# A scan block on one NeuronCore: the tail behind the last pair, reordered over other PSUM banks

## The chip, the core and the metric

The kernel runs on one core of one Trainium2 chip. Its time is the device time of one execution in microseconds (us); lower is better. Five engines work side by side and wait for each other through semaphores: TensorE (PE in the profile, with PEld for its weight loads), VectorE (DVE), ScalarE (ACT), GpSimd (POOL), and SyncE (SP), which issues the transfers. TensorE writes its results to PSUM, which the kernel uses as one tile of eight banks, `psum[128, 8, 512]`. Only VectorE and ScalarE read these banks here; GpSimd works on SBUF alone.

## The reference, cut to what matters

The input `x` is (4, 128, 96, 96). It is group-normalized, read as four sequences of 9216 positions per image (rows forward and reversed, columns forward and reversed), and each sequence goes through one block:

```
t = grouped1x1(x, in_proj)            # 512 channels: u, gate
u = depthwise_conv(silu(u), 5 taps)
s, a, b, c = ssm_in(u), decay(u), tanh(ssm_b(u)), tanh(ssm_c(u))     # 32 channels each
h[l] = a[l] * h[l-1] + b[l] * s[l]    # the recurrence along the sequence
u = u + ssm_out(c * h + d * s)        # 32 -> 256 channels
y = out_proj(mix(u * sigmoid(gate)))  # 256 -> 128
```

The four results are joined by a 1x1 convolution (`fuse`) and added to `x`. The kernel keeps the sum of all four in `acc` and merges mix, out_proj and fuse into one matrix per direction, `w_fin`.

## The kernel before, in words

The work is cut into 384 units: 8 phases (4 images, columns then rows), 6 steps in a phase, 4 interleaved positions `p` in a step, and 2 sequences `s` (one forward, one reversed). Two units that differ only in `s` are a pair; a tile holds N = 384 positions. `pair(t)` runs 192 times. It makes the front of pair t (projection, convolution, `proj`) and the back of pair t - 6: so when the loop ends, six pairs still lack their back. These are pairs 186 to 191, that is units 372 to 383, and `tail()` (L893 to L986) finishes them. The order of the work is written out by hand: each engine executes its instructions in the order in which the code issues them, and a wait holds all that is queued behind it on that engine.

The back of one pair (units bi and bi + 1, with bi even) has these steps; the names are used below.

- **Scan** (`scan`, L702, VectorE): the recurrence over one step's 4 pairs, on partitions 64 to 127 of `t0`, in two halves of 768 elements. The second half starts from the last value of the first.
- **Outputs** (`outputs`, L708 and L709): z = c * h + d * s, a multiplication and an addition over 64 x 384, both of whose inputs lie in SBUF. They run on GpSimd, or on VectorE where `engine` says so.
- **z copy**: z is copied from partitions 0 to 63 to 64 to 127, since the four matmuls that follow use four different groups of 32 rows. It runs on GpSimd (L711, inside `outputs`) or on ScalarE (`z_copy`, L904).
- **Seed** (`under`, L505, ScalarE): u is copied into two PSUM banks, so that the matmuls add onto it.
- **State result** (`out_of`, L497, TensorE, called by `ssm_out` L898): 4 matmuls of 32 rows onto the seeds, for s = 0 into banks SSM and SSM + 1 (0 and 1), for s = 1 into banks 2 and 3.
- **Gating** (`gating`, L577, VectorE; L959 for the last pair in quarters): v = (g + 1) * state result, from the two banks to SBUF. It frees the two banks for the seed of the next pair.
- **Product** (`accumulate`, matmuls of L134 with `w_fin`): 8 matmuls of 32 columns give y of one unit in one bank. The profile counts each float32 matmul twice, so a product shows as 16.
- **Add** (`accumulate`): y goes into `acc`. Either ScalarE copies it to `ys` (L735, L737) and GpSimd adds that (L754), or, where `last` is set, VectorE adds straight from the bank (L752, L754). This frees the product's bank.

In the tail the state results of every pair use banks 0 to 3 and the products banks 4 to 7, in turn (`finish`, L914). The order on TensorE, as the built program has it, is: state result 186, products 370 and 371, state result 187, products 372 to 375, state results 188 and 189, products 376 and 377, state result 190, products 378 and 379, state result 191, products 380 and 381, and units 382 and 383 in four half products. Outputs 376 (pair 188) run on VectorE with their z copy on GpSimd; outputs 378, 380 and 382 run on GpSimd with their z copies on ScalarE. Between the scan's two halves stand state result 187 and the gating of pair 187.

Finished rows of `acc` are sent by `send()` (L717), and the last four pieces by L986.

Of the kernel before, what the change touches and what calls it, by code (L numbers as in the profile page):

```python
# [47 lines left out]
P = 128  # L48
# [14 lines left out]
UB = 8  # L63
# [4 lines left out]
def conv_preact_kernel(  # L68
# [418 lines left out]
    def gate(bi, s, j, to):  # L487
# [3 lines left out]
        nc.tensor.matmul(bank(to)[:, :N], stats[un["b"]][0][r, s, :], x_in[s][r, q, off : off + N],  # L491
                         start=True, stop=True)

    def out_of(bi, s, j):
        z = tbs[bi]
        r = slice(64 * j + 32 * s, 64 * j + 32 * s + 32)
        nc.tensor.matmul(bank(SSM + 2 * s + j)[:, :N], w_so[r, bass.ts(j, P)], z[r, :],  # L497
                         start=bi not in seeded, stop=True, skip_group_check=True)

    seeded = set()  # L500
# [1 line left out]
    def under(bi, s):  # L502

        seeded.add(bi)
        nc.scalar.copy(psum[:, SSM + 2 * s : SSM + 2 * s + 2, :N], us[bi][:, s])  # L505

    def sigmoids(bi, to):
        bn = stats[units[bi]["b"]][1]
# [57 lines left out]
    def gating(bi, s):  # L566

        v = units[bi + s]["v"] = us[bi][:, s]
        m = mirror(bi // 2)
        if m is None:  # L570
            g = gates[bi // 2 % 2][:, s]
        else:
            g = old_gates.get(bi // 2, gates[m % 2])[:, 1 - s, :, ::-1]
        pz = psum[:, SSM + 2 * s : SSM + 2 * s + 2, :N]
        if bi not in seeded:
            nc.vector.tensor_add(pz, pz, v)
        nc.vector.scalar_tensor_tensor(v, g, 1.0, pz, ALU.add, ALU.mult)  # L577
# [125 lines left out]
            seq[64:P, r], seq[64:P, r], seq[0:64, r], init, ALU.mult, ALU.add  # L703
        )

    def outputs(i, copy=nc.gpsimd.tensor_copy, engine=nc.gpsimd):
        ta, tb, p = scans[units[i]["step"]], tbs[i], units[i]["p"]
        engine.tensor_mul(ta[0:64, p, :], tb[64:P, :], ta[64:P, p, :])  # L708
        engine.tensor_add(tb[0:64, :], ta[0:64, p, :], tb[0:64, :])  # L709
        if copy:  # L710
            copy(tb[64:P, :], tb[0:64, :])  # L711

# [180 lines left out]
    def tail():  # L893
# [12 lines left out]
        def gate_units(n):  # L906
            for s in range(2):
                gating(2 * n, s)
                under(2 * n + 2, s)
                if s == 0 and n > first + 1:  # L910
                    z_copy(n + 1)
            waiting.extend(units[2 * n : 2 * n + 2])

        def finish(n):  # L914
            banks = (4, 5) if n % 2 else (6, 7)
            accumulate(waiting.pop(0), banks[0])()
            wait.append(accumulate(waiting.pop(0), banks[1], nc.vector, True))

        def add():
            if wait:  # L920
                wait.pop(0)()
            send()

        z_copy(first + 1)
        ssm_out(first)
        gate_units(first)
        for bk in (4, 5):
            accumulate(waiting.pop(0), bk)()
        scan(NU // UB - 1, 0)
        scale_s(NU - 2)  # L930
        ssm_out(first + 1)
        gate_units(first + 1)
        scan(NU // UB - 1, 1)
        outputs(2 * first + 4, nc.gpsimd.tensor_copy, nc.vector)
        outputs(2 * first + 6, None)
        for bk in (6, 7):
            wait.append(accumulate(waiting.pop(0), bk, nc.vector, True))
        for n in range(first + 4, end):
            outputs(2 * n, None)
        finish(first + 1)  # L940
        add()
        add()
        ssm_out(first + 2)
        for n in range(first + 2, end - 1):
            gate_units(n)
            add()
            if n > first + 2:
                finish(n - 1)
            ssm_out(n + 1)
        last = 2 * (end - 1)  # L950
        half = N // 2
        for s in range(2):
            bu = units[last + s]
            v = us[last][:, s]
            g = old_gates[last // 2][:, 1 - s, :, ::-1]
            for e in range(2):
                r = bass.ts(e, half)
                pz = psum[:, SSM + 2 * s : SSM + 2 * s + 2, r]
                nc.vector.scalar_tensor_tensor(v[:, :, r], g[:, :, r], 1.0, pz, ALU.add, ALU.mult)  # L959
        add()  # L960
        finish(end - 2)
        add()
        for s in range(2):
            bu = units[last + s]
            v = us[last][:, s]
            for e in range(2):
                r = bass.ts(e, half)
                py = bank(4 + 2 * s + e)
                for j in range(2):
                    for c in range(4):  # L970
# [202 lines left out]
```

## Time and profile before

| quantity | value |
|---|---|
| median of 3 runs | 1819.84 us (1818.55 to 1820.01) |
| the profiled execution, its own time | 1821.96 us |
| its span, first to last instruction | 1820.2 us |
| tail on TensorE (first product after pair 191's matmuls to the last matmul's end) | 1783.57 to 1815.24 us |
| last addition into `acc` ends | 1815.66 us |
| TensorE busy from 1784.5 to 1791.3 us | 6.61 of 6.80 us |
| ScalarE, VectorE, GpSimd busy over the span | 86%, 80%, 78% |

A row of the timeline reads: start in us from the span's beginning, duration in us, engine, source line, operation, what it writes and reads, shapes, and count; in brackets the idle time of the engine before it and what ended that time. Successive matmuls of a kind are merged into one row, which lasts from the first start to the last end, so waits inside such a row are not seen as idle time. In the view of windows each row gives a stretch, its length, the busy time and the number of instructions of each engine, and the TensorE clock that was granted (1.00 is full).

### The profile page before, as it was taken

The page shows a single profiled execution, that of the slowest core. Times are in us where ns is not written, and L with a number is a line of the kernel's source. Part 1 is how long each engine was busy: PE and PEld are TensorE (multiplying, and loading weights), DVE is VectorE, ACT ScalarE, POOL GpSimd, SP SyncE. Part 2 cuts the span into 40 slices and gives each one's busy share as a digit, 9 for nine tenths or more (in the row PEclk, how much of TensorE's full clock was granted, in tenths as well). Part 3 has the DMA queues.
Part 4 walks back from the last instruction along what each step waited for, and adds up shares of the span by engine and source line. Part 5 has one row for each costly group of instructions (what it writes and reads, how often), then busy time and mean ns, then how long its engine had stood idle before and what let it go on. Part 6 is the DMA issues. An engine that isn't in the chain of part 4 may idle for free.

```text
span 1820.2 us, 56934 instructions
## 1 busy us (share of the span) xinstructions
PE 1792.3 (98%) x24074; PEld 645.5 (35%) x24074; DVE 1454.6 (80%) x1462; ACT 1562.5 (86%) x2748; POOL 1428.2 (78%) x1475
## 2 busy tenths in 40 slices
PE   6999999999999999999999999999999999999998
PEld 3333333333333333333333333333333333333333
DVE  6888878877888888877778888887877788778885
ACT  4888888988988888888888888888888888888974
POOL 3587878778778888788877888887877888887785
PEclk9999999999999999999999999999999999999999
DMA  8555463444975465334696456453477644635434
GB/s 246 175 190 179 149 203 99 162 142 154 313 242 181 158 196 171 119 135 137 224 296 227 141 179 210 119 171 110 161 237 223 227 148 129 197 102 177 149 125 155
DMA packets 148047, 321.17 MB, mean 176 GB/s; under 512 B 14160, under 2 KB 115920, under 8 KB 147792
## 3 DMA queue, kind: packets, MB, share of 16 engines
q1 hardware_dynamic: 147648, 317.48, 54.2%
q8 instruction: 190, 3.11, 0.7%
q14 instruction: 65, 0.53, 0.1%
q10 hardware_dynamic: 144, 0.04, 0.0%
HBM read 185.21 MB, written 132.25 MB: 174 GB/s over the span
## 4 chain that ended last, share of the span: by engine, by line
PE 94%; ACT 2%; DVE 2%; DMA 1%; issue 0%; SPq 0%; POOL 0%; DVEq 0%; ACTq 0%; POOLq 0%
PE psum L134 81%; PE psum L497 8%; PE psum L491 5%; DMA xs<-in_xr 1%; ACT psum L505 1%; ACT sil L470 1%; DVE psum L630 1%; DMA acc<-in_xr 0%; DVE bn L298 0%; ACT u L611 0%; DVE u L577 0%; DVE u L630 0%; ACT psum L628 0%; DVE t L702 0%; SPq L296 0%
## 5 line engine op out<-in xcount | busy, mean ns | idle before, releaser
L630 DVE SCALAR_TENSOR_TENSOR psum<-sil,small,psum 128x768 f32<-128x768 f32 x576 | 589.0, 1023 | 28.8 <-ACT psum L628 3.4
L134 PE MATMUL psum<-u,w_fin 128*32 128x384 f32 x6176 | 553.1, 488 | 0.2 <-ACT t L673 0.2
L577 DVE SCALAR_TENSOR_TENSOR u<-gate,psum 128x768 f32<-128x768 f32 x376 | 349.8, 952 | 249.0 <-ACT gate L514 107.2
L134 PE MATMUL psum<-u,main 128*32 128x384 f32 x6144 | 534.9, 489 | 1.6 <-DVE u L630 1.5
L754 POOL TENSOR_TENSOR acc<-ys,acc 128x384 f32<-128x384 f32 x374 | 410.7, 1120 | 32.1 <-ACT ys L735 10.8
L708 POOL TENSOR_TENSOR t<-t,t 64x384 f32<-64x384 f32 x191 | 232.3, 1216 | 153.8 <-DVE t L702 70.2
L134 PEld LDWEIGHTS psum<-u,w_fin 128*32 128x32 f32 x6176 | 188.9, 110 | 322.4 <-issue 216.6
L134 PEld LDWEIGHTS psum<-u,main 128*32 128x32 f32 x6144 | 181.9, 109 | 328.4 <-issue 200.7
L505 ACT COPY psum<-u 128x768 f32<-128x768 f32 x352 | 276.7, 799 | 23.1 <-DVE u L630 11.3
L134 PE MATMUL psum<-sil,band 128*32 128x384 f32 x3072 | 285.2, 488 | 0.0
L675 POOL TENSOR_SCALAR t<-tm 64x384 f32<-64x384 f32 x191 | 177.2, 928 | 123.2 <-ACT tm L667 104.2
L709 POOL TENSOR_TENSOR t<-t,t 64x384 f32<-64x384 f32 x191 | 246.8, 1292 | 15.0
L497 PE MATMUL psum<-t,main 32*128 32x384 f32 x1536 | 242.1, 514 | 3.3 <-ACT psum L505 2.6
L628 ACT ACTIVATE psum<-sil,small 128x768 f32<-128x768 f32 x191 | 173.2, 907 | 61.1 <-DVE u L577 52.8
L514 ACT ACTIVATE gate<-psum,bnorm 128x384 f32<-128x384 f32 x384 | 192.1, 582 | 30.1 <-PE psum L491 28.6
L676 POOL TENSOR_TENSOR t<-t,tm 64x384 f32<-64x384 f32 x192 | 195.1, 1016 | 15.3
L630 DVE SCALAR_TENSOR_TENSOR u<-sil,small,psum 128x768 f32<-128x768 f32 x192 | 194.9, 1015 | 7.8
L470 ACT ACTIVATE sil<-psum,bnorm 128x385 f32<-128x385 f32 x384 | 192.1, 585 | 3.7 <-PE psum L134 1.5
L134 PE MATMUL psum<-sil,less 64*32 64x384 f32 x3072 | 168.1, 495 | 0.0
L491 PE MATMUL psum<-x_in,wn 32*128 32x384 f32 x768 | 157.4, 526 | 3.0 <-DVE shift L249 1.4
L711 POOL COPY t<-t 64x384 f32<-64x384 f32 x188 | 141.2, 751 | 15.5 <-PE psum L134 3.6
L134 PEld LDWEIGHTS psum<-sil,band 128*32 128x32 f32 x3072 | 90.3, 109 | 169.6 <-issue 94.4
(102 smaller groups left out, 1484.3 us busy)
## 6 DMA issues: line engine op xcount, KB each, us to landing
sil<-sil SPq DMA_DIRECT2D x128, 770.0 KB, 6.8
kept<-gate SPq DMA_DIRECT2D x80, 768.0 KB, 3.7
gate<-kept SPq DMA_DIRECT2D x76, 768.0 KB, 5.1
x_in<-in_xs SPq DMA_DIRECT2D x192, 96.2 KB, 2.5
out<-acc SPq DMA_DIRECT2D x48, 384.0 KB, 8.0
acc<-in_xr SPq DMA_DIRECT2D x39, 384.0 KB, 6.9
xs<-in_xr SPq DMA_DIRECT2D x72, 192.0 KB, 5.5
x_in<-in_xs SPq DMA_DIRECT2D x46, 192.5 KB, 3.5
```

The source lines that it names most:

```text
L134: nc.tensor.matmul(o[r, : rhs.shape[-1]], lhsT, rhs, start=start, stop=stop, skip_group_check=True)
L470: nc.scalar.activation(sils[step][:, s, j, g, :], bank(bk)[:, : N + 1], AF.Silu, bias=bn[:, 1:2] if j else bn[:, 4 + g : 5 + g],)
L491: nc.tensor.matmul(bank(to)[:, :N], stats[un["b"]][0][r, s, :], x_in[s][r, q, off : off + N], start=True, stop=True)
L497: nc.tensor.matmul(bank(SSM + 2 * s + j)[:, :N], w_so[r, bass.ts(j, P)], z[r, :], start=bi not in seeded, stop=True, skip_group_check=True)
L505: nc.scalar.copy(psum[:, SSM + 2 * s : SSM + 2 * s + 2, :N], us[bi][:, s])
L514: nc.scalar.activation(gv[:, s, j, :], bank(to[2 * s + j])[:, :N], AF.Tanh, bias=bn[:, 2 + j : 3 + j], scale=0.5,)
L577: nc.vector.scalar_tensor_tensor(v, g, 1.0, pz, ALU.add, ALU.mult)
L630: nc.vector.scalar_tensor_tensor(us[i][:, :, 1, :] if k == K - 1 else part, src, w_tap[:, k : k + 1], part, ALU.mult, ALU.add,)
L676: nc.gpsimd.tensor_mul(ta[0:64, p, :], tb[0:64, :], tm[0:64, :])
L708: engine.tensor_mul(ta[0:64, p, :], tb[64:P, :], ta[64:P, p, :])
L709: engine.tensor_add(tb[0:64, :], ta[0:64, p, :], tb[0:64, :])
L754: adder.tensor_add(part, y, part)
```

## The change

Everything outside `tail()` issues the same instructions as before. In the tail:

- The state results of the last four pairs (188 to 191) turn through three pairs of banks, 6 and 7, 0 and 1, 2 and 3, one pair of banks for each unit (`ssm`). The products use banks 4 and 5 alone, 4 for s = 0 and 5 for s = 1.
- The two halves of the last scan stand together, ahead of the gating of pair 187. Behind each half follow the outputs of 376 for that half of the positions, on GpSimd.
- Outputs 378 move from GpSimd to VectorE. The z copy of 376 moves from GpSimd to ScalarE.
- GpSimd's addition of 371 is issued behind the outputs of 376 instead of ahead of them.
- Product 372 no longer goes straight from the bank through VectorE, but through ScalarE's `ys` and a GpSimd addition, as all s = 0 products now do; s = 1 products are added by VectorE.
- On TensorE, state results and products alternate: 372, 373, 374, state result 188, 375, 376, state result 189, 377, 378, state result 190, 379, 380, state result 191, 381, then the four half products, in banks 4, 2, 3 and 6.
- On ScalarE each z copy stands behind both seeds of its pair.

```diff
+    turning = (6, 0, 2)
+    def ssm(bi, s):
+        k = bi - NU + 8 + s
+        return turning[k % 3] if bi >= NU - 8 else SSM + 2 * s
...
-        nc.tensor.matmul(bank(SSM + 2 * s + j)[:, :N], w_so[r, bass.ts(j, P)], z[r, :],
+        nc.tensor.matmul(bank(ssm(bi, s) + j)[:, :N], w_so[r, bass.ts(j, P)], z[r, :],
...
-    def outputs(i, copy=nc.gpsimd.tensor_copy, engine=nc.gpsimd):
+    def outputs(i, copy=nc.gpsimd.tensor_copy, engine=nc.gpsimd, r=slice(0, N)):
...
-        engine.tensor_mul(ta[0:64, p, :], tb[64:P, :], ta[64:P, p, :])
-        engine.tensor_add(tb[0:64, :], ta[0:64, p, :], tb[0:64, :])
+        engine.tensor_mul(ta[0:64, p, r], tb[64:P, r], ta[64:P, p, r])
+        engine.tensor_add(tb[0:64, r], ta[0:64, p, r], tb[0:64, r])
...
-                if s == 0 and n > first + 1:
-                    z_copy(n + 1)
-            waiting.extend(units[2 * n : 2 * n + 2])
-
-        def finish(n):
-            banks = (4, 5) if n % 2 else (6, 7)
-            accumulate(waiting.pop(0), banks[0])()
-            wait.append(accumulate(waiting.pop(0), banks[1], nc.vector, True))
+
+        def product(n, s, bk):
+            if s == 0:
+                accumulate(units[2 * n], bk)()
+            else:
+                wait.append(accumulate(units[2 * n + 1], bk, nc.vector, True))
...
         gate_units(first)
-        for bk in (4, 5):
-            accumulate(waiting.pop(0), bk)()
-        scan(NU // UB - 1, 0)
+        first_add, second_add = (accumulate(waiting.pop(0), bk) for bk in (4, 5))
+        first_add()
         scale_s(NU - 2)
+        for part in range(2):
+            scan(NU // UB - 1, part)
+            outputs(2 * first + 4, None, r=bass.ts(part, N // 2))
         ssm_out(first + 1)
+        second_add()
         gate_units(first + 1)
-        scan(NU // UB - 1, 1)
-        outputs(2 * first + 4, nc.gpsimd.tensor_copy, nc.vector)
-        outputs(2 * first + 6, None)
-        for bk in (6, 7):
-            wait.append(accumulate(waiting.pop(0), bk, nc.vector, True))
+        outputs(2 * first + 6, None, nc.vector)
+        product(first, 0, 4)
+        product(first, 1, 5)
+        z_copy(first + 2)
+        product(first + 1, 0, 4)
         for n in range(first + 4, end):
             outputs(2 * n, None)
-        finish(first + 1)
-        add()
         add()
         ssm_out(first + 2)
         for n in range(first + 2, end - 1):
             gate_units(n)
+            z_copy(n + 1)
+            product(n - 1, 1, 5)
             add()
-            if n > first + 2:
-                finish(n - 1)
+            product(n, 0, 4)
             ssm_out(n + 1)
...
-        add()
-        finish(end - 2)
+        product(end - 2, 1, 5)
         add()
...
-                py = bank(4 + 2 * s + e)
+                py = bank((4, 2, 3, 6)[2 * s + e])
```

More of the change, by code (lines that the diff above doesn't have):

```diff
@@ L504, in under @@
         seeded.add(bi)
-        nc.scalar.copy(psum[:, SSM + 2 * s : SSM + 2 * s + 2, :N], us[bi][:, s])
+        nc.scalar.copy(psum[:, ssm(bi, s) : ssm(bi, s) + 2, :N], us[bi][:, s])
     def sigmoids(bi, to):
@@ L573, in gating @@
             g = old_gates.get(bi // 2, gates[m % 2])[:, 1 - s, :, ::-1]
-        pz = psum[:, SSM + 2 * s : SSM + 2 * s + 2, :N]
+        pz = psum[:, ssm(bi, s) : ssm(bi, s) + 2, :N]
         if bi not in seeded:
@@ L909, in gate_units @@
                 under(2 * n + 2, s)
-                if s == 0 and n > first + 1:
-                    z_copy(n + 1)
-            waiting.extend(units[2 * n : 2 * n + 2])
-        def finish(n):
-            banks = (4, 5) if n % 2 else (6, 7)
-            accumulate(waiting.pop(0), banks[0])()
-            wait.append(accumulate(waiting.pop(0), banks[1], nc.vector, True))
+        def product(n, s, bk):
[3 more added lines that the diff above has]
+                wait.append(accumulate(units[2 * n + 1], bk, nc.vector, True))
         def add():
-            if wait:
-                wait.pop(0)()
+            wait.pop(0)()
             send()
@@ L957, in tail @@
                 r = bass.ts(e, half)
-                pz = psum[:, SSM + 2 * s : SSM + 2 * s + 2, r]
+                pz = psum[:, ssm(last, s) : ssm(last, s) + 2, r]
                 nc.vector.scalar_tensor_tensor(v[:, :, r], g[:, :, r], 1.0, pz, ALU.add, ALU.mult)
-        add()
-        finish(end - 2)
+        product(end - 2, 1, 5)
         add()
```

## The prediction

> **What bounds the kernel now.** I read the page's busy shares and chain first:
>
> ```profile
> span 1820.2 us, 56934 instructions
> ...
> PE 94%; ACT 2%; DVE 2%; DMA 1%; issue 0%; SPq 0%; POOL 0%; DVEq 0%; ACTq 0%; POOLq 0%
> ```
>
> TensorE is the chain for 94% of the span; outside the tail it is busy almost without a break, and the change leaves that part alone. So the question is what TensorE does behind pair 191. Its timeline there:
>
> ```profile
> 1788.07 5.37 PE L134 MATMUL psum<-u,w_fin 128*32 128x384 f32 x64
> 1793.44 1.49 PE L497 MATMUL psum<-t,main 32*128 32x384 f32 x8
> 1796.95 2.79 PE L497 MATMUL psum<-t,main 32*128 32x384 f32 x8 [2.02 <-ACT psum L505]
> 1799.66 5.35 PE L134 MATMUL psum<-u,w_fin 128*32 128x384 f32 x32
> 1804.94 0.93 PE L497 MATMUL psum<-t,main 32*128 32x384 f32 x8
> 1805.80 2.79 PE L134 MATMUL psum<-u,w_fin 128*32 128x384 f32 x32
> 1808.52 1.41 PE L497 MATMUL psum<-t,main 32*128 32x384 f32 x8
> 1809.85 5.39 PE L134 MATMUL psum<-u,w_fin 128*32 128x384 f32 x96
> ```
>
> Four products (x64) take 5.37 us, so one takes 1.29 us; a state result that waits for nothing holds TensorE for 0.86 us (1804.94 to 1805.80). Behind state result 188 TensorE has nothing left: result 189 needs the banks that gating 188 has yet to read. It idles 2.02 us and is then held again inside the row of 1796.95. And two products that take 2.79 us at 1805.80 took 5.35 us at 1799.66. The view of windows says why:
>
> ```profile
> 1791.30:1794.70 3.40, 3.39 (x36) 1.25 (x28) 2.92 (x5) 0.58 (x1) 1.17 (x2) 1.00 0.31 125
> 1794.70:1798.10 3.40, 1.38 (x9) 0.60 (x6) 2.28 (x3) 2.01 (x3) 3.17 (x4) 1.00 0.02 5
> 1798.10:1805.00 6.90, 6.90 (x41) 1.94 (x40) 1.91 (x2) 2.63 (x4) 5.25 (x5) 0.51 0.25 95
> ```
>
> The column behind the last bracket is the granted clock. After a stretch with TensorE busy for 1.38 of 3.40 us (41%) it ran at half clock for 6.9 us, which costs half of that, 3.4 us.
>
> **What could be had.** From 1788.07 the work is ten products (12.9), four state results (3.4) and four half products (2.6), with about 0.3 for the last matmul to end: 19.2 us, done at 1807.3. It ended at 1815.24 (1809.85 + 5.39). So 7.9 us are lost: 3.4 to the clock, 4.5 to waits. Nothing in the change can gain more.
>
> **The change, part by part.**
>
> *Alternation and turning banks.* With products 375 and 376 between state results 188 and 189, TensorE has 2 x 1.29 = 2.58 us of work while the chain to the next state result runs. That chain is gating of s = 0 (0.95), seed (0.80), z copy and TensorE's wake-up:
>
> ```profile
> 1796.00 0.80 ACT L505 COPY psum<-u 128x768 f32<-128x768 f32 x1 [3.21 <-DVE u L577]
> 1796.83 0.51 ACT L904 COPY t<-t 64x384 f32<-64x384 f32 x1
> ```
>
> The matmul of 1796.95 starts 0.15 us after that seed ends. So 0.05 + 0.95 + 0.05 + 0.80 + 0.03 + 0.51 + 0.15 = 2.54 us, hidden by 2.58 with nothing to spare; I allow 0.05 us of waiting in each of three rounds. The seed of s = 0 goes to banks already free and is done before. Bank 5 is freed by VectorE's additions (0.55), which end a microsecond before the next product needs it, bank 4 by `ys` (0.58) likewise. Under these covers both cost nothing.
>
> *Product 374* is the exception. It needs bank 4, and the `ys` of 372 stands on ScalarE behind the seed of 376 s = 1, which now waits for gating 374, which stands behind the second scan half. By rows: scan halves 1785.43 to 1787.25 and 1787.28 to 1789.1, gating to 1790.1, seed to 1791.0, `ys` to 1791.6, product 374 at 1791.7 instead of 1790.65: about 1 us of TensorE. What comes next swallows it.
>
> *Outputs 376 on GpSimd.* This is what decides. The four half operations have no row. Rows of GpSimd at other sizes:
>
> ```profile
> L226 POOL TENSOR_TENSOR inv<-inv,err 128x2 f32<-128x2 f32 x9 | 1.8, 196 | 0.7
> L1057 POOL TENSOR_TENSOR w_of<-w_of 128x512 f32<-128x512 f32 x1 | 1.3, 1278 | 8.0 <-ACT sil L470 8.0
> L1057 POOL TENSOR_TENSOR w_of<-w_of 128x256 f32<-128x256 f32 x1 | 0.7, 737 | 0.1
> ```
>
> These lie on a line from a base of 0.196 us. A whole output operation takes 1.19 (L708 in the tail), so a half is bounded by 0.60 (no base) and 1.19 (all base), and I take 0.196 + 0.99/2 = 0.69 us, with gaps of 0.08. Beside them stands this, from an earlier step:
>
> ```profile
> 1752.51 1.19 POOL L709 TENSOR_TENSOR t<-t,t 64x384 f32<-64x384 f32 x1
> 1752.52 2.80 DVE L702 TENSOR_TENSOR_SCAN t<-t,t 64x768 f32<-64x768 f32 x1
> 1753.77 1.86 POOL L711 COPY t<-t 64x384 f32<-64x384 f32 x1
> ```
>
> The scan, 1.81 us alone, took 2.80: it stood until GpSimd's operation ended. The copy, 0.50 alone, took 1.86: it stood until the scan ended, and finished 0.3 us later (its own time less 0.2). A scan and a GpSimd operation take turns. In the tail before, GpSimd had almost nothing to do beside the second half and VectorE's outputs. Now:
>
> - GpSimd's addition of 370, ready at 1787.85, stands until the scan ends at 1789.1, and ends at 1789.1 + 1.0 - 0.2 = 1789.9.
> - First half: multiplication to 1790.7, addition to 1791.45.
> - VectorE's outputs of 378 (0.89 each) come up at 1791.05. Whether they too take turns with GpSimd no row shows: the lower bound is no hold (gating rows beside GpSimd keep their 0.95), the upper that of the scan. I take turns, since like the scan they read two operands from SBUF and the gating reads one. So VectorE multiplies to 1792.15, GpSimd to 1792.65, VectorE adds to 1793.35, GpSimd to 1793.85. Without turns it would be 1793.0.
>
> The GPSIMD Engine Reference, Key points, says the same in general: GpSimd shares its SBUF interfaces with VectorE, with contention where VectorE reads two inputs from SBUF. By that rule 1814.5 us comes out, by free running 1813.7.
>
> Then the z copy ends at 1794.4, the waiting matmuls go on at 1794.55, and TensorE is free for 375 at 1795.4. Before, state result 188 ended at 1794.93; it comes no earlier now. The gain comes from what follows it.
>
> *The rest.* From 1795.4: five products (6.45), three state results (2.58), three waits (0.15), then two products and the four halves as before (5.39): 1795.4 + 14.57 = 1809.97. Before: 1815.24. The difference is **5.3 us**. Behind the last matmul everything stays: additions, the last transfers, 5.0 us to the span's end. On GpSimd three additions (1.08 each with the gap) and outputs 380 and 382 (1.27 an operation) follow 1793.85, so these end at 1799.6 and 1802.2; their z copies are due near 1800.8 and 1804.5. The transfers of finished rows move earlier and collide with nothing: the last ones still wait for the last additions.
>
> The span falls from 1820.2 to 1814.9; the profiled execution (1821.96, 1.7 us around the span) stands 2.1 us above the median. Taken from the median: 1819.84 - 5.3 = **1814.5 us** (-0.29%). A measurement of this kernel can tell about 0.2% (3.6 us) from no change.
>
> **The rivals.**
>
> *Half clock again.* In the window from 1791.3 to 1794.7 TensorE has product 374 (1.5 us) and the first part of state result 188 (0.7): busy about 65%. Below is the 41% that lost the clock; above, an early stretch that kept it:
>
> ```profile
> 16.40:19.80 3.40, 2.41 (x6) 0.78 (x5) 3.23 (x7) 0.00 (x0) 0.00 (x0) 1.00 1.05 286
> ```
>
> That is 71%. 65% is nearer to that, but no row tells which stretches the clock gate weighs. If the clock falls once: 1814.5 + 3.4 = 1817.9 us, no difference that counts. The same would come near if halves cost whole operations (up to 1.2 to 2.6 us more). The page TensorE: Matmul & The Clock Gate has the throttle fall only after an idle window of about 3.4 us; the trace lost its clock with 2.02 us idle at most, so the measurement decides. But its section "A second HAM failure mode: psum-queue depth-cycling" speaks against this change: turning through PSUM banks left TensorE with micro-idles and a clock that swung. By that section the sum would be 1817.9 or more.
>
> *GpSimd and VectorE do not hold each other up.* Then outputs 376 end at 1793.0 with only the scan's hold, giving 1813.7; with no hold at all at 1792, product 374 is the only wait, giving 1812.9.
>
> *Slower: the clock stays half.* If each round leaves TensorE below the share that lost the clock, three stretches of 6.9 us in a row cost 10.2 us: 1814.5 + 10.2 = 1824.7. It decides from the third stretch on (two give 1821.3). Against it: in the half-clock stretch before, TensorE was busy 6.90 of 6.90 us and got the clock back; a round of 3.44 us at full clock lasts 6.9 at half, and its other chain 2.54, so TensorE would be kept full again.
>
> **How the numbers follow.** Forecast (1813.8 to 1816.2, with the bounds of the half operation that keep the clock): 0.61. Half clock once (1816.3 to 1819): 0.23. No holds (1812.8 to 1813.7): 0.12. Slower: 0.04. Range 1812.8 to 1818.3: it takes in the first, the third and most of the second. Faster by over 0.2% needs 1816.2 or less: the first and third, 0.73; same 0.23; slower 0.04.
>
> **What would show it.** In the profile after: state result 188 held between its first and its other matmuls by a z copy that ends near 1794.4; GpSimd's half operations at about 0.69 us, some lasting longer beside VectorE's L715 and L716; product 374 about 1 us after 373; no idle time on TensorE above 0.2 us behind 375; clock 1.00 to the last matmul; that matmul's end near 1810. A half-clock window behind 1794, or a z copy behind 1795.5, makes the prediction wrong.

## The result, and the profile after

| | before | after |
|---|---|---|
| median | 1820.07 us (22 runs, 1818.34 to 1827.76) | **1816.69 us** (22 runs, 1815.58 to 1823.06) |
| ratio, 95% interval | | **0.9983** [0.9977, 0.9989] |
| profiled execution: span | 1820.2 us | 1816.9 us |
| start of state result 186 | 1782.54 us | 1784.16 us |
| tail: from there to the last matmul's end | **32.71 us** | **27.59 us** |
| last matmul's end to the end of the span | 5.0 us | 5.15 us |

The change makes the kernel 3.4 us faster between the medians (0.19%), 0.17% by the ratio, whose interval stays below 1. Forecast were 1814.5 us and a range of 1812.8 to 1818.3: the range holds the time, the forecast is 2.2 us too low, and the gain lies at the 0.2% that I had called the bound of what can be told. A second set of 12 runs of the changed kernel, beside other runs of the one before, gave 0.9978 [0.9968, 0.9988].

The page of the changed kernel, span and chain:

```profile
span 1816.9 us, 56940 instructions
...
PE 93%; ACT 2%; DMA 2%; POOL 1%; DVE 1%; issue 0%; SPq 0%; POOLq 0%; DVEq 0%
```

TensorE still is the chain; GpSimd has come into it with 1%. TensorE's timeline in the tail (start, duration, and in brackets the idle time ahead):

```profile
1789.67 2.79 PE L134 MATMUL psum<-u,w_fin 128*32 128x384 f32 x32
1793.10 1.50 PE L134 MATMUL psum<-u,w_fin 128*32 128x384 f32 x16 [0.64 <-ACT ys L742]
1795.53 1.46 PE L504 MATMUL psum<-t,main 32*128 32x384 f32 x8 [0.94 <-POOL t L716]
1796.93 2.79 PE L134 MATMUL psum<-u,w_fin 128*32 128x384 f32 x32
1799.64 0.93 PE L504 MATMUL psum<-t,main 32*128 32x384 f32 x8
1800.50 2.79 PE L134 MATMUL psum<-u,w_fin 128*32 128x384 f32 x32
...
1807.65 4.10 PE L134 MATMUL psum<-u,w_fin 128*32 128x384 f32 x80
```

Two waits stand where they were predicted: product 374 (1793.10, for `ys`) and state result 188 (1795.53, for the outputs of 376), whose row lasts 1.46 us instead of 0.93 because it is held once more after its first matmuls, until the z copy of 376 ends at 1796.02. From 1796.93 on there is no bracket: each round of two products and a state result takes 3.57 us. The view of windows (granted clock behind the last bracket; the last two columns are the busy share of the DMA engines and the GB/s that they moved):

```profile
1791.30:1794.70 3.40, 2.66 (x32) 0.68 (x24) 3.33 (x4) 1.31 (x2) 3.09 (x5) 1.00 0.84 336
1794.70:1798.10 3.40, 2.57 (x24) 1.02 (x25) 1.83 (x4) 1.88 (x4) 3.40 (x4) 1.00 0.01 5
1798.10:1811.75 13.65, 13.65 (x189) 5.82 (x184) 9.29 (x16) 7.00 (x11) 8.05 (x8) 1.00 0.34 128
```

TensorE was busy for 78% and 76% of the two stretches with the waits, kept the full clock in both, and then worked 13.65 of 13.65 us.

But this execution lost a clock elsewhere. The same stretch near the start, first of the changed kernel:

```profile
25.00:31.60 6.60, 6.60 (x70) 4.50 (x54) 0.93 (x5) 4.62 (x10) 0.83 (x1) 0.50 0.30 78
```

and of the kernel before:

```profile
25.00:31.60 6.60, 6.60 (x128) 4.01 (x116) 2.73 (x11) 6.34 (x14) 2.64 (x3) 1.00 0.39 93
```

The instructions there are the same; the change has no part in it. In this execution state result 186 starts 1.62 us later than before; in another of the same kernel, with full clock there, it starts 2.5 us earlier than in this one (experiment 12). So the two tails are compared from the start of state result 186, and moments of the changed kernel are set against the forecast less 1.62 us.

### The profile page after: what moved, and what is told of

Read it like the earlier page. It is cut to its first block, busy times and chain, and to the rows that moved or that the text cites. A ratio compares the mean times of both kernels' runs of the same rounds, so it can differ in the third digit from the quotient of the medians.

```text
span 1816.9 us, 56940 instructions
## 1 busy us (share of the span) xinstructions
PE 1790.3 (99%) x24074; PEld 645.7 (36%) x24074; DVE 1454.2 (80%) x1461; ACT 1563.5 (86%) x2750; POOL 1429.9 (79%) x1477
## 4 chain that ended last, share of the span: by engine, by line
PE 93%; ACT 2%; DMA 2%; POOL 1%; DVE 1%; issue 0%; SPq 0%; POOLq 0%; DVEq 0%
PE psum L134 80%; PE psum L504 8%; PE psum L491 5%; DMA x_in<-in_xs 1%; DMA xs<-in_xr 1%; ACT sil L470 1%; ACT psum L512 1%; POOL t L715 0%; POOL t L716 0%; DMA acc<-in_xr 0%; DVE psum L637 0%; POOL acc L761 0%; ACT u L618 0%; PE psum L1012 0%; POOL t L683 0%
## 5 line engine op out<-in xcount | busy, mean ns | idle before, releaser
L761 POOL TENSOR_TENSOR acc<-ys,acc 128x384 f32<-128x384 f32 x375 | 412.8, 1122 | 26.7 <-ACT ys L744 7.4
L715 POOL TENSOR_TENSOR t<-t,t 64x384 f32<-64x384 f32 (+1 forms) x192 | 233.1, 1214 | 154.2 <-DVE t L709 70.4
L716 POOL TENSOR_TENSOR t<-t,t 64x384 f32<-64x384 f32 (+1 forms) x192 | 247.0, 1286 | 15.1
```

The source lines that it names most:

```text
L715: engine.tensor_mul(ta[0:64, p, r], tb[64:P, r], ta[64:P, p, r])
L716: engine.tensor_add(tb[0:64, r], ta[0:64, p, r], tb[0:64, r])
L761: adder.tensor_add(part, y, part)
```

## The experiments

Each kernel's profile is read the same way: the tail, and the starts of state results 188 to 191 and product 375, all counted from the start of state result 186. Before: 188 at 10.91, 189 at 14.41, tail 32.71. Changed: 188 at 11.38, 375 at 12.77, 189 at 15.49, then rounds of 3.57, tail 27.59.

**1. The kernel before, again** (`b_again`, no edit).

> The kernel before, once more, to see whether its profiled execution was a usual one. Theory (clock): the stretch at half clock is not the same in each execution, so this profile's tail (start of state result 186 to the end of the last matmul) differs from the 32.7 us of the first profile by up to 3.4 us, and the runs' spans spread over 2 us or more, the shorter ones with a granted clock nearer to 1.000. Rival (fixed cost): the tail is 32.7 us again with the half clock at the same place, and the spans lie within 1 us of 1820.2.

Measured: 1820.47 us, ratio 0.9995 [0.9982, 1.0008], tail 31.12 us. The windows around state result 189:

```profile
1794.50:1797.90 3.40, 2.08 (x12) 0.98 (x16) 2.36 (x4) 2.01 (x3) 3.22 (x3) 1.00 0.02 5
1797.95:1801.30 3.35, 3.35 (x24) 1.10 (x23) 1.08 (x2) 2.53 (x4) 3.27 (x3) 0.50 0.00 0
```

Again a half clock behind the idle time, this time for 3.41 us instead of 6.83. The same instructions, in the same order, lost about 1.7 us here and 3.4 us in the first profile. The price of the half clock differs between executions of one kernel. The 12 runs spread over 5.4 us (1819.25 to 1824.69); the two longest have the lowest granted clock, 0.996 against 0.997 to 0.999.

**2. The clock alone** (`e_filler`): the kernel before with three matmuls into a free bank where TensorE idled.

```diff
             if n > first + 2:
                 finish(n - 1)
+            else:
+                for _ in range(3):
+                    nc.tensor.matmul(bank(6)[:, :N], w_fin[:, 0, 0, :],
+                                     units[2 * first + 3]["v"][:, 0, :], start=True, stop=True)
             ssm_out(n + 1)
```

> The kernel before with three matmuls more on TensorE (128 x 128 x 384, 0.64 us each by the time of a product's half, into bank 6, which nothing reads until product 376 overwrites it) between state results 188 and 189, where TensorE idled 2.02 us. Theory (the share of busy time of that stretch lost the clock): no half clock in the tail, products 376 and 377 take 2.8 us instead of up to 5.4, and the tail is 29.3 us (32.71 less 3.4); in time 1.7 to 3.4 us below the kernel before, since the half clock costs that in its executions: 1816.7 to 1818.4 us. Rival (the half clock comes for another reason, such as the banks): the half clock stays and the tail is 32.7 us or longer.

Measured: tail **29.40 us**, 1817.68 us, ratio 0.9989 [0.9980, 0.9998]. TensorE's rows:

```profile
1799.95 1.48 PE L497 MATMUL psum<-t,main 32*128 32x384 f32 x8
1801.37 2.20 PE L951 MATMUL psum<-u,w_fin 128*128 128x384 f32 x6
1803.50 2.01 PE L497 MATMUL psum<-t,main 32*128 32x384 f32 x8
1805.44 2.79 PE L134 MATMUL psum<-u,w_fin 128*32 128x384 f32 x32
```

The fillers (L951) fill the gap between state results 188 and 189, and the two products behind them take 2.79 us, not 5.35. Work that computes nothing makes the kernel faster, by 0.1%, with an interval that just stays below 1. So 32.71 - 29.40 = 3.3 us of the first profile's tail were clock.

**3. The order without the banks** (`e_bank`): the changed kernel, state results of all pairs in banks 0 to 3.

```diff
-        return turning[k % 3] if bi >= NU - 8 else SSM + 2 * s
+        return SSM + 2 * s
...
-                py = bank((4, 2, 3, 6)[2 * s + e])
+                py = bank((4, 6, 7, 5)[2 * s + e])
```

> The changed kernel with its new order, but the state results of the last four pairs in banks 0 to 3 as before instead of turning through three pairs of banks (the four half products in banks 4, 6, 7 and 5). Theory (turning is what hides the chain): the seed of s = 0 must wait for the gating of s = 0, the seed of s = 1 for that of s = 1, and the z copy stands behind both: 0.05 + 1.90 + 0.05 + 0.80 + 0.51 + 0.15 = about 3.4 us, of which two products hide 2.58, so each of three rounds waits 0.8 us: tail 30.0 us (27.59), about 1819.2 us; TensorE stays above 75% busy and the clock at 1.00. Rival (alternation alone gives the gain): tail 27.6 us, 1816.7 us.

Measured: tail **29.46 us**, 1818.55 us, ratio 0.9997 [0.9985, 1.0008].

```profile
1800.56 2.79 PE L134 MATMUL psum<-u,w_fin 128*32 128x384 f32 x32
1803.28 1.54 PE L504 MATMUL psum<-t,main 32*128 32x384 f32 x8
1804.75 2.79 PE L134 MATMUL psum<-u,w_fin 128*32 128x384 f32 x32
1807.46 1.54 PE L504 MATMUL psum<-t,main 32*128 32x384 f32 x8
```

Each state result is held inside its row (1.54 instead of 0.93), a round takes 4.19 us, 0.61 more than with turning banks (I had 0.8). The granted clock is 1.00 to the last matmul. So in the tail alternation alone does what the fillers do (29.46 beside 29.40), and turning through three pairs of banks is worth the other 1.87 us. The time does not show the first part: with a ratio of 0.9997 this kernel can't be told from the one before. The profiled execution ran at half clock for 13.65 us near its start (21.94 to 35.59 us), outside the tail.

**4. Order and banks without the scan part** (`p_alt`): scan halves, outputs 376 on VectorE and their z copy as before, 378 on GpSimd.

```diff
+        second_add()
+        scan(NU // UB - 1, 0)
         scale_s(NU - 2)
-        for part in range(2):
-            scan(NU // UB - 1, part)
-            outputs(2 * first + 4, None, r=bass.ts(part, N // 2))
         ssm_out(first + 1)
-        second_add()
         gate_units(first + 1)
-        outputs(2 * first + 6, None, nc.vector)
+        scan(NU // UB - 1, 1)
+        outputs(2 * first + 4, nc.gpsimd.tensor_copy, nc.vector)
+        outputs(2 * first + 6, None)
...
-        z_copy(first + 2)
```

> The new order on TensorE with its banks, but the last scan as before: its halves apart, outputs 376 on VectorE, their z copy on GpSimd, outputs 378 on GpSimd. Theory (the alternation is the gain, and outputs 376 on GpSimd are what state result 188 waits for): product 375 starts about 12.3 us after state result 186 instead of 12.8 in the changed kernel, the tail lasts about 27.1 us instead of 27.6, and the time is 0.4 us below the changed kernel's, ratio to before near 0.998. Rival (the scan halves together are the gain): the tail is nearer to before's 32.7 us than to 27.6, ratio 0.9995 or more.

Measured: tail **27.56 us**, 1816.73 us, ratio 0.9974 [0.9964, 0.9985]: all of the gain. Product 375 starts at 12.25 as expected, 0.5 us ahead of the changed kernel's; yet the tail is no shorter, against my 27.1. The half microsecond is given back at state result 190, which is held for outputs 380, since on GpSimd these come behind two additions (TensorE's row of 190, then GpSimd's):

```profile
1800.94 1.42 PE L504 MATMUL psum<-t,main 32*128 32x384 f32 x8
...
1796.29 1.96 POOL L761 TENSOR_TENSOR acc<-ys,acc 128x384 f32<-128x384 f32 x2
1798.32 1.23 POOL L715 TENSOR_TENSOR t<-t,t 64x384 f32<-64x384 f32 x1
1799.63 1.22 POOL L716 TENSOR_TENSOR t<-t,t 64x384 f32<-64x384 f32 x1
```

**5. The scan part alone** (`p_scan`): order and banks as before.

```diff
-        for bk in (4, 5):
-            accumulate(waiting.pop(0), bk)()
-        scan(NU // UB - 1, 0)
+        first_add, second_add = (accumulate(waiting.pop(0), bk) for bk in (4, 5))
+        first_add()
         scale_s(NU - 2)
+        for part in range(2):
+            scan(NU // UB - 1, part)
+            outputs(2 * first + 4, None, r=bass.ts(part, N // 2))
...
```

> The regrouped scan alone: its halves together with outputs 376 in halves on GpSimd, 378 on VectorE, z copy 376 on ScalarE; TensorE's order and banks as before. Theory: state result 188 ends 0.3 to 0.9 us later than before and TensorE idles behind it as before, so the tail is as long as before or up to 1 us longer, ratio 0.9995 to 1.0005. Rival (the scan halves together are the gain): tail under 30 us, ratio 0.9985 or less.

Measured: 1820.94 us, ratio 1.0003 [0.9991, 1.0015]; tail 32.39 us with 6.83 us of half clock; state result 188 comes 0.6 us later than before. This part brings nothing that can be told.

**6. Turns between GpSimd and VectorE** (`e_gp378`): the changed kernel with outputs 378 on GpSimd, behind those of 376.

```diff
-        second_add()
         gate_units(first + 1)
-        outputs(2 * first + 6, None, nc.vector)
+        outputs(2 * first + 6, None)
+        second_add()
```

> The changed kernel with outputs 378 back on GpSimd, behind those of 376, and the addition of 371 behind them. Theory (VectorE's outputs and GpSimd take turns): all four half operations take 0.67 to 0.70 us (two took 1.24 and 1.03), z copy 376 comes 0.9 us earlier, the tail is 26.7 us against 27.6. Rival (the second halves are slow for a reason of their own): they stay above 1 us, and the tail stays at 27.6 us or grows.

First GpSimd in the changed kernel, behind the addition of 370 (L761):

```profile
1789.46 2.06 POOL L761 TENSOR_TENSOR acc<-ys,acc 128x384 f32<-128x384 f32 x1 [3.17 <-ACT ys L742]
1791.60 0.70 POOL L715 TENSOR_TENSOR t<-t,t 64x192 f32<-64x192 f32 x1
1792.38 0.67 POOL L716 TENSOR_TENSOR t<-t,t 64x192 f32<-64x192 f32 x1
1793.13 1.24 POOL L715 TENSOR_TENSOR t<-t,t 64x192 f32<-64x192 f32 x1
1794.45 1.03 POOL L716 TENSOR_TENSOR t<-t,t 64x192 f32<-64x192 f32 x1
```

and VectorE beside it, second scan half and outputs 378:

```profile
1788.90 1.81 DVE L709 TENSOR_TENSOR_SCAN t<-t 64x768 f32<-64x768 f32 x1
...
1792.60 1.21 DVE L715 TENSOR_TENSOR t<-t,t 64x384 f32<-64x384 f32 x1
1793.84 1.15 DVE L716 TENSOR_TENSOR t<-t,t 64x384 f32<-64x384 f32 x1
```

The addition of 370 (0.98 alone) is held until the scan is over at 1790.71 and ends 0.81 us behind it. Half operations take 0.70 and 0.67 while VectorE gates, and 1.24 and 1.03 while it runs outputs 378. With these on GpSimd, in `e_gp378`:

```profile
1791.05 0.70 POOL L715 TENSOR_TENSOR t<-t,t 64x192 f32<-64x192 f32 x1
1791.83 0.68 POOL L716 TENSOR_TENSOR t<-t,t 64x192 f32<-64x192 f32 x1
...
1795.04 2.93 POOL L761 TENSOR_TENSOR acc<-ys,acc 128x384 f32<-128x384 f32 x3
...
1799.36 1.20 POOL L716 TENSOR_TENSOR t<-t,t 64x384 f32<-64x384 f32 x1
```

the second halves are as fast as the first (0.70 and 0.68, shown above) and product 375 starts at 11.89, 0.88 us earlier, as expected. So the holds are real. But the tail is 27.60 us, not 26.7 (1816.27 us, ratio 0.9976 [0.9964, 0.9989]): again state result 190 is held, as outputs 380 stand behind three additions:

```profile
1800.60 1.46 PE L504 MATMUL psum<-t,main 32*128 32x384 f32 x8 [0.28 <-POOL t L716]
```

**7. Those additions out of the way** (`e_gp380`): as 6, with outputs 380 and 382 also ahead of all additions but the first.

```diff
         gate_units(first + 1)
-        outputs(2 * first + 6, None)
+        for n in range(first + 3, end):
+            outputs(2 * n, None)
         second_add()
...
-        for n in range(first + 4, end):
-            outputs(2 * n, None)
```

> The changed kernel with outputs 378 on GpSimd behind outputs 376, followed at once by outputs 380 and 382, and all additions from 371 on behind these: the kernel of the run e_gp378 with the additions out of the way. Theory (there state result 190 was held because outputs 380 stood behind three additions): product 375 at 11.9 as in e_gp378, state results 190 and 191 not held, tail 26.7 us (27.60 in e_gp378), about 1815.8 us. Rival (190 was held by something else): 190 is held again and the tail stays at 27.6 us.

Measured: tail **26.77 us**, 190 and 191 not held: GpSimd's queue was the cause in 6, and by the same rows in 4. The time does not follow: 1817.07 us, ratio 0.9988 [0.9978, 0.9999]. What was gained ahead of the last matmul is lost behind it: 6.4 us to the end of the span instead of 5.15. Experiments 9 to 11 say why.

**8. The wait of product 374** (`e_ys372`): the changed kernel with the `ys` of 372 ahead of the seeds of 376 on ScalarE.

```diff
-        gate_units(first + 1)
+        gating(2 * first + 2, 0)
+        third_add = accumulate(units[2 * first], 4)
+        under(2 * first + 4, 0)
+        gating(2 * first + 2, 1)
+        under(2 * first + 4, 1)
         outputs(2 * first + 6, None, nc.vector)
-        product(first, 0, 4)
+        third_add()
```

> The changed kernel with the ys of 372 alone moved ahead of the seeds of 376 on ScalarE. Theory (the wait of product 374 is swallowed by the z copy of 376, which comes from GpSimd): product 374 starts without the 0.64 us of idle time, but state result 188 still waits for the same z copy, product 375 starts at 12.8 as before, tail 27.6 us, 1816.7 us. Rival (ScalarE's order sets the end): product 375 comes 0.6 us earlier and the tail is 27.0 us, 1816.1 us.

Measured: 374 no longer waits, state result 188 starts at 11.39 and product 375 at 12.78, both unchanged: the wait was swallowed, as forecast. But the tail of this execution is 29.26 us, a miss. TensorE, and the windows:

```profile
1798.83 1.46 PE L504 MATMUL psum<-t,main 32*128 32x384 f32 x8 [1.78 <-POOL t L716]
1800.22 4.44 PE L134 MATMUL psum<-u,w_fin 128*32 128x384 f32 x32
```

```profile
1796.79:1800.19 3.40, 1.62 (x12) 0.60 (x8) 1.92 (x3) 1.36 (x3) 3.32 (x4) 1.00 0.14 54
1800.20:1803.60 3.40, 3.40 (x27) 1.17 (x28) 2.34 (x3) 1.73 (x3) 3.24 (x4) 0.50 0.34 126
```

The two waits of the changed kernel (0.64 and 0.94 us, with product 374 between them) have become one of 1.78. In the stretch ahead of 1800.2 TensorE was busy for 1.62 of 3.40 us (48%), and the clock fell for 3.41 us. This is one profiled execution; the median (1817.13 us, ratio 0.9985 [0.9974, 0.9996]) doesn't tell whether others lose it too.

**9. GpSimd's queue put in the order in which TensorE needs it** (`best`): outputs 376 unsplit and with nothing ahead, 378, addition 370, outputs 380, addition 371, outputs 382, then the rest; `ys` 372 early as in 8.

```diff
-        first_add()
         scale_s(NU - 2)
         for part in range(2):
             scan(NU // UB - 1, part)
-            outputs(2 * first + 4, None, r=bass.ts(part, N // 2))
+        outputs(2 * first + 4, None)
         ssm_out(first + 1)
+        outputs(2 * first + 6, None)
+        first_add()
+        outputs(2 * first + 8, None)
         second_add()
-        gate_units(first + 1)
-        outputs(2 * first + 6, None, nc.vector)
...
```

> The changed kernel with a new order on GpSimd: outputs 376 start at the scan's end with nothing ahead of them, then outputs 378 (also on GpSimd), the addition of 370, outputs 380, the addition of 371, outputs 382, and all other additions behind these; the ys of 372 stands on ScalarE ahead of the seeds of 376. Theory (the bound behind the change is GpSimd's queue): outputs 376 end 2.5 us behind the scan (9.1 us behind the start of state result 186), their z copy at 9.8, state result 188 is held only until 9.9, product 375 starts at 10.8 (12.77 in the changed kernel), product 374 doesn't wait, state results 189 to 191 are not held; tail 25.6 us (27.59), so 1814.7 us, 2.0 below the changed kernel. Rival (the tail is bound by the chain of gating, seed and z copy): each of the three rounds gains waits instead and the tail stays above 27 us. TensorE busy all the time, so no half clock in the tail.

Measured: tail **25.46 us**, product 375 at 10.63, no wait behind it, no half clock: 2.1 us less than the changed kernel. The time is 1815.93 us, ratio 0.9981 [0.9971, 0.9991], no different from the changed kernel's. From the last matmul (1805.71) to the end of the span (1812.9) it now takes 7.2 us. SyncE's transfers out in this kernel (start of the first issue, time until the last, count):

```profile
1801.04 2.31 SPq L724 DMA_DIRECT2D out<-acc  x4
1804.54 3.16 SPq L995 DMA_DIRECT2D out<-acc  x4
```

and in the changed kernel:

```profile
1798.40 3.18 SPq L724 DMA_DIRECT2D out<-acc  x4
1810.58 2.31 SPq L991 DMA_DIRECT2D out<-acc  x4
```

Four transfers of finished rows (384 KB each) used to leave 12 us ahead of the last four; now they leave 3.5 us ahead. The windows of the transfers, two of this kernel and then one of the changed kernel:

```profile
1802.00:1806.00 4.00, 3.71 (x80) 2.30 (x72) 3.48 (x9) 0.00 (x0) 1.94 (x2) 1.00 1.03 393
1806.00:1810.00 4.00, 0.00 (x0) 0.00 (x0) 0.13 (x1) 0.00 (x0) 0.00 (x0) 0.99 0.93 361
```

```profile
1804.00:1811.00 7.00, 7.00 (x112) 3.43 (x112) 5.44 (x10) 2.60 (x4) 2.46 (x3) 1.00 0.02 5
```

In `best` the DMA engines work through all eight transfers almost without a pause, at 393 and 361 GB/s; in the changed kernel they had finished the first four by 1804 and then moved 5 GB/s until the last four left.

**10. One addition earlier** (`best2`): the kernel of 9 with addition 374 in the place of that of 371 on GpSimd (and five buffers for `ys` instead of four).

```diff
-        second_add()
-        outputs(2 * first + 10, None)
...
-        third_add()
...
         product(first + 1, 0, 4)
+        outputs(2 * first + 10, None)
+        second_add()
+        third_add()
```

> The kernel of the run best with one move on GpSimd: the addition of 374, which releases the transfer of finished rows, stands ahead of outputs 382 in the place of that of 371 (so ys has 5 buffers instead of 4). In the run best the tail was 25.46 us but 7.2 us lay between the last matmul and the end of the span, against 5.15 in the changed kernel, and two sends of finished rows (4 transfers) were issued together at 1801.04 us, just ahead of the last four. Theory (the transfers that came late behind the addition of 374 hold up the last ones): with that addition early the stretch behind the last matmul is 5.1 to 5.3 us again, tail 25.5 us, time 2.1 us below the changed kernel, about 1814.5 us. Rival (the longer stretch has nothing to do with these transfers): it stays at 7 us, and the time at 1815.9 us.

Measured: tail 25.45 us, 1816.07 us, ratio 0.9979 [0.9970, 0.9987]; 7.2 us behind the last matmul. The move did not make the transfers earlier: they were issued at 1802.44, 20.8 us behind the start of 186 and 3.5 us ahead of the last four, just as in 9 (not 0.8 us ahead, as the expectation of experiment 11 has it). The rows that they send also take the additions of 371 and 372, and these still stood behind outputs 382. The experiment tested nothing but that.

**11. All those additions earlier** (`best3`): outputs 382 on VectorE, one operation in each of two rounds, so that GpSimd adds 371, 372 and 374 at once behind outputs 380.

```diff
+        on_vector = [
+            lambda: nc.vector.tensor_mul(ta[0:64, p, :], tb[64:P, :], ta[64:P, p, :]),
+            lambda: nc.vector.tensor_add(tb[0:64, :], ta[0:64, p, :], tb[0:64, :]),
+        ]
...
+            if on_vector:
+                on_vector.pop(0)()
             product(n, 0, 4)
```

> In the run best2 the transfers of finished rows still left 0.8 us ahead of the last four (the addition of 374 was early, that of 372, which belongs to the same rows, was not), and 7.2 us still lay behind the last matmul. Here outputs 382 go to VectorE, one operation behind each of two additions of s = 1, where VectorE idled 1.3 us in a round; GpSimd runs outputs 376 and 378, the addition of 370, outputs 380 and then all other additions, so 371, 372 and 374 end 18.2 us behind the start of state result 186 instead of 20.8. Theory (those transfers hold up the last ones): they are issued at 18.2 to 18.8, 5 us ahead of the last four, the stretch behind the last matmul is 5.1 to 5.5 us, the tail 25.5 to 25.8, the time about 1.8 us below the changed kernel: 1814.5 us. Rival (the longer stretch has another reason): it stays at 7 us and the time at 1816 us.

Measured: 1817.10 us, ratio 0.9978 [0.9968, 0.9988], beside runs of the kernel before that themselves were higher (1821.37 us). The stretch behind the last matmul is **5.16 us** again, with the transfers of finished rows issued 7.8 us ahead of the last four (1807.30 and 1815.08): the first half of the theory holds, late transfers of finished rows hold up the last ones. In `best`, `best3` and the changed kernel alike the last four are first issued 1.2 us ahead of the last matmul's end, so what differs lies behind that. But the tail is 27.71 us, not 25.8. VectorE's rows for outputs 382:

```profile
1801.59 1.73 DVE L952 TENSOR_TENSOR t<-t,t 64x384 f32<-64x384 f32 x1
...
1805.56 3.29 DVE L953 TENSOR_TENSOR t<-t,t 64x384 f32<-64x384 f32 x1
```

beside GpSimd's

```profile
1802.64 1.74 POOL L716 TENSOR_TENSOR t<-t,t 64x384 f32<-64x384 f32 x1
1804.34 5.32 POOL L761 TENSOR_TENSOR acc<-ys,acc 128x384 f32<-128x384 f32 x5
```

The two operations take 0.87 and 0.84 us where GpSimd is idle (experiment 4). Beside GpSimd's queue of additions the second took 3.29: not one turn but several, since three of the additions (about 1.0 us each) ended between its start and its end. The gating behind it came late, TensorE idled 1.62 us ahead of product 380.

**12. The changed kernel again** (`a_again`, no edit).

> The changed kernel again, beside the runs of this call. Theory: tail 27.6 us, no half clock in it, 5.1 us behind the last matmul, median 1816.7 us; 186 starts 1.6 us earlier than in the first profile if the start of the execution loses no clock. Rival (the gain was luck of one execution): a half clock in the tail in this one, and a median above 1818.

Measured: 1816.25 us, ratio 0.9978 [0.9968, 0.9988]; tail 27.60 us, no half clock in it; state result 186 at 1781.65, with full clock near the start, 2.5 us earlier than in the first profile where I had expected 1.6; span 1814.4 us.

## Why the prediction was right, and where it was wrong

**The tail, step by step.** Moments of the changed kernel, less the 1.62 us by which this execution was late, beside the forecast:

| step | forecast | measured |
|---|---|---|
| addition of 370 ends, held by the scan | 1789.9 | 1789.90 |
| product 374 starts | 1791.7 | 1791.48 |
| half operations on GpSimd, alone | 0.69 | 0.70, 0.67 |
| outputs 376 end, with turns | 1793.85 | 1793.86 |
| z copy ends | 1794.4 | 1794.40 |
| product 375 starts | 1795.4 | 1795.31 |
| idle time behind 375, each round | 0.05 | none |
| clock to the last matmul | 1.00 | 1.00 |
| last matmul ends | 1809.97 | 1810.13 |

The z copy on which all this hangs:

```profile
1795.51 0.51 ACT L911 COPY t<-t 64x384 f32<-64x384 f32 x1 [2.47 <-POOL t L716]
```

The tail shrank by 5.12 us, forecast were 5.3. One price in it was misread: "Four products (x64) take 5.37 us, so one takes 1.29". A quarter of 5.37 is 1.34; 1.29 is what each further product adds to a row ((5.37 - 2.79) / 2). Two products between state results hold TensorE for 2.71 us (1796.93 to 1799.64), not 2.58, and the prediction's own rows showed 2.72 (1805.80 to 1808.52). So a round takes 3.57 us, not 3.49, though it has no wait, and the stretch from product 375 to the last matmul's end 14.82 us, not 14.57.

The estimate for half operations, read off a line through other sizes, was within 0.02 us. Of the two views on VectorE and GpSimd, turns were right; free running would have had outputs 376 end at 1793.0. The Trainium skill's GPSIMD Engine Reference, Key points, says that VectorE instructions with two SBUF inputs contend with GpSimd; the rows here agree (1.24 and 1.03 beside 1.21 and 1.15, against 0.70 and 0.89 undisturbed).

**What gave the gain.** In the profiled tails, from 32.71 to 29.4 us it is the clock, whether fillers (29.40) or alternation (29.46) keep TensorE busy; from there to 27.6 it is the banks. Each of these tails is one execution, except that the changed kernel's was seen twice (27.59 and 27.60). The scan part gives nothing by itself (experiment 5) and is not missed (4). I had written that state result 188 "comes no earlier now" and that the gain comes behind it; that was right.

**The rivals.** *Half clock again* did not come: TensorE was busy 78% and 76% where I had reckoned 65%. Experiment 8 did lose the clock, behind a stretch with one wait instead of two and 48% busy. But the busy share is not the whole rule, as this stretch of `best3` shows:

```profile
1807.01:1810.42 3.41, 1.79 (x24) 0.60 (x20) 3.41 (x3) 1.02 (x2) 2.65 (x3) 1.00 0.69 268
```

TensorE was busy for 53% of it, idled 1.62 us in one piece, and kept the full clock to the last matmul. So why the half clock stayed away is not shown. The Trainium skill's TensorE: Matmul & The Clock Gate, "A second HAM failure mode: psum-queue depth-cycling", had spoken against turning banks; of nine profiles of kernels that turn them, eight show 1.00 through the tail, and only that of experiment 8 does not, whose banks are those of the changed kernel. The same page, "What's actually happening", ties the fall to an idle window of about 3.4 us; experiment 8 fell with 1.78 us idle in one piece, so the measurement decides.

**The step that failed** is the last one, "Taken from the median: 1819.84 - 5.3". The mechanism was right; the term that was mis-sized is the clock, put at 3.4 us of the median. The 5.3 us were worked out against one execution that had paid 6.83 us of half clock and stood 2.1 us above the median: a price was taken off that not every execution pays in full. Experiment 1 shows what was missed: another execution of the same kernel paid 1.7 us. With that price the gain is 5.3 - 1.7 = 3.6 us, and 1820.07 - 3.6 = 1816.5. This is an estimate from few executions: the run `p_scan`, whose tail has the same wait, paid 6.83 us again, and what share of all pays which price, the runs do not show.

That 1821.96 - 5.3 = 1816.7 comes close to the median of 1816.69 is luck. The 2.1 us were not all clock: state result 186 started at 1782.54 in that execution and at 1781.40 and 1781.07 in `b_again` and `p_scan`, all three with full clock from 17.1 us up to there. And the changed kernel's own profiled execution took 1818.64 us.

The time also fell outside the interval of the forecast (1813.8 to 1816.2, chance 0.61) and into that of "half clock once" (1816.3 to 1819, chance 0.23), although no half clock came in the tail. So the number fell where another cause had been expected, and the range held it because it was drawn to take in most of that rival.

**What stays open.** No experiment beat the changed kernel by more than can be told: `best` and `best2` have 2.1 us less on TensorE and lose as much to transfers behind it; `best3` mends the transfers and loses 2.2 us to turns. A kernel with both was not tried. What decides whether the clock falls is not settled: near the start of the changed kernel's execution it fell right behind this stretch, with TensorE busy for 95% of it (73% of the one before):

```profile
21.52:24.93 3.41, 3.23 (x97) 1.76 (x105) 1.07 (x7) 2.61 (x6) 0.00 (x0) 1.00 0.72 175
```

Nor is it settled why the half clock lasts 3.41 us in one execution and 6.83 in another, and why only some executions lose it near the start. One thing the clock records of all fourteen traces do show: each stretch of one clock that ends within the trace lasts a whole number of steps of 3.413 us (3.413, 6.827, 10.240, 13.653, 17.067; the long ones 517 to 527 steps), and the steps lie elsewhere in the program in each execution (the clock fell 15.59 us behind the start of state result 186 before, 16.52 in `b_again`, 14.33 in `p_scan`). So the price comes in steps of about 1.7 us.

## What to carry to other kernels

Before a difference worked out from one trace is taken from a median, ask of each term whether every execution pays it, and a clock penalty is the first suspect: a second profile of the same kernel told here. Where TensorE must wait, put work that is ready between dependent matmuls and give their results enough banks for the next seed to be written while the last is still read: here the first kept the clock, the second hid the chain, and they could be priced apart by fillers and by fixed banks. When one queue stops being the bound, look at the order of the next: here GpSimd's outputs, its additions and the transfers that wait for these each took back what the step before had won.

## What the runs showed of the hardware that was not expected

- The clock can fall after a stretch in which TensorE was busy for 41% (before), 48% (`e_ys372`) or 61% (`b_again`: 2.08 of 3.40 us), with at most 2.02 us idle in one piece. The busy share of the stretch just ahead does not decide alone: the clock stayed full behind one with 53% (`best3`) and fell behind one with 95% (the changed kernel, near its start), both shown above. The stretch at half clock lasted 3.41 or 6.83 us in the tail, and up to 13.65 us near the start of an execution (25.83 to 39.48 us in `e_filler`'s), with the same instructions in each.
- Turn-taking is not limited to one turn: a VectorE addition over 64 x 384 with both inputs in SBUF took 0.84 us alone, 1.15 to 1.21 beside one GpSimd operation, and 3.29 us beside a queue of GpSimd additions that followed each other closely.
- Four transfers of 384 KB that leave 3.5 us ahead of the last four make the end of the span come 2 us later (7.2 us behind the last matmul instead of 5.15); 4.4 us ahead, in `e_gp380`, 1.3 us later.
